# Attention with sorted limits: limits on GpSimd, four scalings on VectorE, and twelve products moved behind a branch

## The chip, the core and the metric

The kernel runs on one core of a Trainium2 chip. A core has five engines that run their own instruction lists and meet only at semaphores: TensorE (PE in the profile; PEld is its weight load), VectorE (DVE), ScalarE (ACT), GpSimd (POOL) and SyncE (SP), which here only issues DMAs. The metric is the device time of one execution in microseconds (us). Less is better.

## The reference

A decoder layer on 16 sequences of 256 tokens with 512 channels, f32: selective self-attention, a cross-attention, a feed-forward part, each followed by a residual add and a layer norm. Only the self-attention matters here:

```python
q_I = (x @ W_Iq).reshape(Bx, Tx, IH, DI); k_I = (x @ W_Ik).reshape(Bx, Tx, IH, DI)    # IH = 4
w = sigmoid(x @ W_Iw)
imp = w * sigmoid(einsum('bthd,bshd->bhts', q_I, k_I) + gate_bias)
imp = repeat(imp, H // IH, axis=1) * sigmoid(head_bias)                               # H = 16
k_t = clip(floor(K_BASE * var(causal imp) / variance_ema), K_MIN, K_MAX)
...
sel = the k_t keys of highest imp in each row (the first 4 keys always), causal
q, k = rotary(x @ W_q), rotary(x @ W_k);  v = x @ W_v * sigmoid(x @ W_gv)
attn = softmax(where(sel, q k^T / sqrt(32), -1e30))
out = (attn @ v) * sigmoid(x @ W_go) @ W_o
```

Each row of each head so has its own number of keys, and keeps those with the highest importance.

## The kernel before

**Stages.** After constants, `gates` (to about 343 us) computes w in a chain of exact products. `gate_sums` closes it: the sigmoid of w on VectorE, and beside it `project(0)`, the projections of the first sequence. Then `attention` computes, from w and the head bias, how many sorted keys any row can need, loads that flag into every engine (`values_load`, line 460) and branches to one of two bodies (`attend_all`, lines 461 to 464), which differ in the depth of the sort; the profiled execution takes the one of 64. From about 386 to 1790 us the body runs, then come the cross-attention and the feed-forward part, which the change does not touch.

**Projections.** `project(b)` is a generator. It makes 18 products in a fixed order: Iq, Ik, four of q, four of k, two of gv, four of go, two of v. Each takes two steps: the matmuls (a piece P of the plan), and ACT's copy out of PSUM (a piece C, line 599 or 643). After the fourth copy of q or k two DMAs on SP's queue (line 620) write the swapped pairs to `rot`, and three GpSimd instructions follow, one at each of the next copies: times cos (L621), rot times sin (L622), the add (L623), each over 128x1024. Sequence 0 is projected as a whole ahead of the branch; each later sequence in the slots of the sequence before it.

**Units.** A unit is one sequence with one of the four index heads, 64 in all; it serves four attention heads. Its work is cut into pieces that stand for: L logits (PE); G the gate, first on VectorE (L660), then Exp on ACT (L663), then plus one on GpSimd (L665); I reciprocal (VectorE, L673), times w (GpSimd, L677), statistics (VectorE, L683 to L688) and u (GpSimd, L690); V the four scalings of u by a head's factor, one piece per head (`scaled`, L704: 128x384, f32); R the sort with MAX8 and MATCH_REPLACE8 (L716, L718); N the counts (seven small GpSimd instructions, L726 to L733); T the thresholds (hits L749 on VectorE, L753 on GpSimd, then L757 to L773 with kseen); K the signs against the threshold (ACT, L781, with a sum per row); B the limit, `signs - k` (`limits`, L788, 8 elements a row); X and D transposes and the dropped keys (D on ACT, L815, takes the limit as bias); S scores; M maxima (L834); E exponentials (L842); Z scaling of p by 1/total (GpSimd, L851, eight instructions); A transposes of p and the product with v; U avs (ACT) times go (GpSimd, avT, L883); O the output projection, xs add (GpSimd, L898) and norm.

**Order.** The text `PLAN` (lines 54 to 59) is the order of one slot: `R1:3` is piece 1 of the sort for unit n+3. `attend_all` writes it out for slots n from -4 on and skips what doesn't exist yet, so that a slot holds pieces of several units; `in_order` then pins this order on PE, VectorE, ACT and GpSimd. SP keeps its own order of issue. A piece P or C in slot n advances the projection of sequence n//4 + 1 by one step, at position n%4 * 5 + k of its 18 products. In slots -4 to -1 there is nothing to do for P and C, since sequence 0 is already projected (`if 0 < b < B`, line 488). So n%4 tells which products and which norms lie in a slot: 0 the products from Iq to the third of q, and the norms of the sequence before; 1 the last of q and four of k, with q's rotation; 2 two of gv and three of go, with k's rotation; 3 the last of go and two of v.

The pieces around the change stand so in the plan:

```
R1:3 Z2:0 V2:2 P0:0 D2:1 V3:2 Z3:0 D3:1 C0:0 ... R2:3
... K3:2 S:1 ... M0:1 G1:4 X0:2 M1:1 T0:3 A4:0 U0:0 B:2 G2:4 O7:-2 U1:0 C2:0
I0:4 R6:3 ...
```

On VectorE, `V3` so comes behind `V2` with nothing between, and `B` stands between hits (T0) and the reciprocal (I0). On GpSimd, `V3` lies between the p scalings Z2 and Z3, and `B` comes ahead of gate L665 (G2). The fourth scaling (`j == 3`) is on GpSimd, the other three are on VectorE; the limit is on VectorE.

**Buffers.** Pool `pj` has two buffers per name unless a count is given, `p1` one. Sequence 0 takes Iq, Ik, qT, kT, goT and v from `p1`, later ones from `pj`. All xT come from one buffer in `xp`, so a sequence's load waits until the products of the one before are done.

Of the kernel before, what the change touches and what calls it, by code (L numbers as in the profile page):

```python
# [20 lines left out]
P = 128  # L21
# [5 lines left out]
KC = C // P  # L27
# [21 lines left out]
W_STEPS = (2.0**-9, 2.0**-17, 2.0**-25)  # L49
GS, GB = 8, 24  # L50
PIECES, SLOTS = 18, 5
VBUFS = 1

PLAN = """
# [8 lines left out]
class Kernel:  # L63
# [177 lines left out]
    def gate_steps(self, st, ps, c):  # L241
        nc, v = self.nc, self.nc.vector
        p1 = self.pool("g1", 1, stack=st)
        p2 = self.pool("g2", 2, stack=st)
        raw = {}
        for n in range(2):
            raw[n] = self.gate_load(p2, n)
        self.steps = self.t(p1, [P, 3], "gsteps")
        for k in range(3):
            v.memset(self.steps[:, k : k + 1], 1.5 * TWO23 * X_STEPS[k])  # L250
        self.minus = self.t(p1, [P, P], "minus", BF16)
        v.tensor_scalar_mul(self.minus, self.ident, -1.0)
        coef = self.gate_weights(p1)
        self.maskf = self.t(p1, [P, 32], "gmaskf")
        v.tensor_reduce(self.maskf, self.ident.rearrange("p (a q) -> p q a", a=4), AX.X, ALU.add)
        self.mask = self.t(p1, [P, 32], "gmask", BF16)
        v.tensor_copy(self.mask, self.maskf)
        big = self.t(ps, [P, C], "big")
        rest, t = (self.t(p1, [P, C], n) for n in ("rest", "t"))
        steps = C // 4  # L260
        starts = [0] + list(range(GS, steps, GB))
        blocks = [[self.t(p1, [P, GS, P], f"bd_first{k}", BF16) for k in range(5)]]
        for k in range(5):
            shape = [P, GS, 32, IH]
            v.tensor_tensor(
                blocks[0][k].rearrange("p j (q h) -> p j q h", h=IH),
                coef[k][:, 0:GS, :].unsqueeze(2).to_broadcast(shape),
                self.mask.unsqueeze(1).unsqueeze(3).to_broadcast(shape), op=ALU.mult)

        def new_block():  # L270
            blocks.append([self.t(p1, [P, GB, P], f"bd{k}", BF16, bufs=2) for k in range(5)])
            return self.gate_blocks(blocks[-1], coef, starts[len(blocks) - 1])

        def new_parts(n):
            parts[n] = self.t(p2, [P, GS, C], "xl", BF16, bufs=3)
            return self.gate_parts(p2, ps, raw.pop(n) if n in raw else self.gate_load(p2, n), parts[n])

        parts = {}
        for step in new_parts(0):
            pass  # L280
        stack = ExitStack()
        for ins in self.rounded:
            stack.enter_context(self.tc.issue_after(ins.ins))
        ahead = new_block(), new_parts(1)
        for n in range(20):
            next(ahead[0], None)
            if n % 3 == 2:
                next(ahead[1], None)
        for step in ahead[1]:
            pass  # L290
        stack.close()
        first = len(nc.cur_bb.bb.instructions)
        work = []
        self.W = {}
        loads = "W_Iq", "W_Ik", "W_q", "W_k", "W_gv", "W_go", "W_v"
        place = lambda j: (0, j) if j < GS else (1 + (j - GS) // GB, (j - GS) % GB)
        small = [self.gate_small(ps, blocks, place(0), parts[0], 0)]
        for j in range(steps):
            n, i = divmod(j, GS)
            if i == GS - 1 and n < len(loads):  # L300
                self.load_weight(loads[n])
            if j == 10 * GS:
                self.load_attention_constants(self.wp)
            if j == 12 * GS:
                self.xT0 = self.load_xT(0)
            if i == 0 and n + 2 < steps // GS:
                work.append(new_parts(n + 2))
            m, at = place(j)
            if at == 0 and m + 1 < len(starts):
                if m:  # L310
                    work.append(new_block())
            for k in range(2):
                self.add(big, blocks[m][k][:, at, :], parts[n][:, i, :], j == 0 and k == 0)
            if j + 1 < steps:
                small.append(self.gate_small(ps, blocks, place(j + 1), parts[(j + 1) // GS], (j + 1) % GS))
            if j == 0:
                v.tensor_copy(t, small.pop(0))
            else:
                v.tensor_add(t, rest, small.pop(0))  # L319
            v.tensor_add(c, t, big)  # L320
            if j + 1 < steps:
                v.tensor_sub(rest, c, big)  # L322
            work = [step for step in work if next(step, None)]
        self.in_order(first)
# [78 lines left out]
    def gate_sums(self, lanes):  # L403


        nc = self.nc
        v = nc.vector
        NO = NT * IH
        self.proj = {}
        made = self.project(0)  # L410
        step = lambda: next(made, None)
        with ExitStack() as st:
            pool = self.pool("g3", 1, stack=st)
            z = self.t(pool, [P, NO + H], "z")
            nc.scalar.dma_start(z[:, NO:], self.rows("head_bias", H))
            l5 = lanes.rearrange("p (n g l h) -> p l g n h", n=4, g=8, l=4)
            a, b = (self.t(pool, [P, 8, 4, IH], n) for n in ("za", "zb"))
            v.tensor_add(a, l5[:, 0], l5[:, 1])
            v.tensor_add(b, l5[:, 2], l5[:, 3])
            v.tensor_add(z[:, 0:NO].rearrange("p (g n h) -> p g n h", g=8, h=IH), a, b)  # L420
            self.load_weight("W_o")
            self.sigmoid(pool, z, self.wc, NO + H)
            for _ in range(2 * PIECES):
                step()
        self.first = self.proj[0]

    def load_x(self, pool, src):
# [38 lines left out]
    def attend_all(self, depth):  # L466

        self.depth = depth
        first = len(self.nc.cur_bb.bb.instructions)
        self.units = [(b, i) for b in range(B) for i in range(IH)]
        self.proj, self.sel = {0: self.first}, {}
        self.made = [self.project(b) for b in range(B)]
        plan = [(w[0], int("0" + w[1 : w.index(":")]), int(w[w.index(":") + 1 :])) for w in PLAN.split()]
        places = [off for _, _, off in plan]
        for n in range(min(-IH, -max(places)), len(self.units) - min(places)):
            for kind, k, off in plan:
                self.piece(kind, k, n + off)  # L480
        self.in_order(first)

    def piece(self, kind, k, n):

        if kind in "PC":

            b, at = n // IH + 1, n % IH * SLOTS + k
            if 0 < b < B and at < PIECES:
                next(self.made[b])
            return  # L490
        if not 0 <= n < len(self.units):
# [73 lines left out]

        self.nc.tensor.matmul(out, lhsT, rhs, start=start, stop=True, skip_group_check=True)  # L566

    def load_xT(self, b):
        xT = self.t(self.xp, [P, KC, T], "xT")
        self.nc.sync.dma_start(xT, self.ap["xT"].rearrange("(c p) n -> p c n", p=P)[:, :, b * T : (b + 1) * T])  # L570
        return xT

    def project(self, b):

        nc, W = self.nc, self.W
        v, g = nc.vector, nc.gpsimd
        r = self.proj[b] = {}
        pool = self.pj if b else self.p1
        if b == 0:
            xT = self.xT0  # L580
        else:
            xT = self.load_xT(b)
        gate = self.t(self.pj, [P, 2, C], "gate", bufs=1)
        later = []

        def product(name, c):
            ps = self.t(self.ps, [P, T], "mm", bufs=2)
# [12 lines left out]
            if later:  # L600
                later.pop(0)()

        for name in ("Iq", "Ik"):
            r[name] = self.t(pool, [P, T], name)
            ps = product(name, 0)
            yield
            copy(r[name], ps)
            yield
        turn = lambda a: a.unsqueeze(1).to_broadcast([P, KC, T])
        for name in ("q", "k"):  # L610
            out = r[name] = self.t(pool, [P, KC, T], name + "T")
            for c in range(KC):
                ps = product(name, c)
# [2 lines left out]
                if c == KC - 1:  # L616

                    rot = self.t(self.pj, [P, KC, T], "rot", bufs=1)
                    for k in range(2):
# [2 lines left out]
                                  lambda a=rot: g.tensor_mul(a, a, turn(self.sin)),  # L622
                                  lambda a=out, b=rot: g.tensor_add(a, a, b)))  # L623
                yield
        for i in range(2):
            ps = rows("gv", i)
            yield
            copy(gate[:, i, :], ps)
            yield
# [68 lines left out]
    def scaled(self, sel, j):  # L698

        if j == 0:  # L700
            sel["vv"] = self.t(self.sp, [P, HPI, SEG], "vv", bufs=VBUFS)
        h = sel["i"] * HPI + j
        eng = self.nc.gpsimd if j == 3 else self.nc.vector
        eng.tensor_scalar(sel["vv"][:, j, :], sel["u"], self.chf[:, h : h + 1], TINY,  # L704
                          op0=ALU.mult, op1=ALU.max)

    def sort(self, sel, part, parts):
# [75 lines left out]
                                      accum_out=sel["signs"][:, s, j : j + 1])  # L783

    def limits(self, sel):
        v = self.nc.vector
        sel["limit"] = self.t(self.sp, [P, 2, HPI], "limit")
        v.tensor_sub(sel["limit"], sel["signs"], sel["k"])  # L788

# [805 lines left out]
```

## Time and profile before

| | us |
|---|---|
| median of three runs | 3102.8 (3097.0 to 3104.5) |
| the profiled execution | 3102.2 |
| its span, first to last instruction | 3100.4 |
| `gates` | to 343 |
| sequence 0's products on PE | 343.5 to 383.2 |
| first reciprocal of the body | 386.6 |
| attention body | to about 1790 |
| cross-attention, feed-forward part | to 2400, to 3100 |
| four units in the middle (timeline, limit to limit) | 85.0 or 85.7, in turn |

The page's first part gives each engine's busy time and its share of the span. The second cuts the span into 40 slices of 77.5 us; a digit is the busy share in tenths. Windows give busy time per engine between two moments. In a timeline each line has start, duration, engine, line of the source, operation, the tile written and read, and, in brackets, how long the engine had been idle and what ended that. An instruction that cannot get at its data shows as a longer duration, not as idle time.

### The profile page before, as it was taken

The page shows a single profiled execution, that of the slowest core. Times are in us where ns is not written, and L with a number is a line of the kernel's source. Part 1 is how long each engine was busy: PE and PEld are TensorE (multiplying, and loading weights), DVE is VectorE, ACT ScalarE, POOL GpSimd, SP SyncE. Part 2 cuts the span into 40 slices and gives each one's busy share as a digit, 9 for nine tenths or more (in the row PEclk, how much of TensorE's full clock was granted, in tenths as well). Part 3 has the DMA queues.
Part 4 walks back from the last instruction along what each step waited for, and adds up shares of the span by engine and source line. Part 5 has one row for each costly group of instructions (what it writes and reads, how often), then busy time and mean ns, then how long its engine had stood idle before and what let it go on. Part 6 is the DMA issues. An engine that isn't in the chain of part 4 may idle for free.

```text
span 3100.4 us, 47026 instructions
## 1 busy us (share of the span) xinstructions
PE 2580.9 (83%) x15194; PEld 1511.3 (49%) x15270; DVE 2380.1 (77%) x6186; ACT 1829.9 (59%) x5175; POOL 1563.2 (50%) x2313
## 2 busy tenths in 40 slices
PE   5676849999999999999999757787876899798887
PEld 1222435656665665665566345555644444343333
DVE  6888599999999999999999467755453544577775
ACT  6765147877777877878777622454342444544442
POOL 5543247777777777777777424454333111012222
PEclk8999969999999999999999878888977899899999
DMA  3532100010010000001000053100100633233341
GB/s 100 140 110 64 41 9 16 35 35 35 28 35 35 35 28 21 32 31 35 35 35 28 15 191 125 39 1 5 25 21 14 232 149 142 109 109 136 113 145 55
DMA packets 85071, 200.83 MB, mean 65 GB/s; under 512 B 14160, under 2 KB 24144, under 8 KB 80720
## 3 DMA queue, kind: packets, MB, share of 16 engines
q1 hardware_dynamic: 69856, 148.17, 14.5%
q10 hardware_dynamic: 9840, 32.78, 3.2%
q0 software_dynamic: 5120, 16.78, 1.3%
q8 instruction: 123, 2.02, 0.3%
q14 instruction: 132, 1.08, 0.1%
HBM read 105.41 MB, written 58.72 MB: 53 GB/s over the span
## 4 chain that ended last, share of the span: by engine, by line
DVE 51%; PE 23%; issue 11%; POOL 10%; ACT 3%; DMA 2%; SPq 0%; DVEq 0%; ACTq 0%; POOLq 0%
PE mm L562 10%; DVE rest L718 9%; PE up L562 7%; DVE lists L716 7%; DVE gate L673 5%; DVE nmax L834 4%; DVE W_o L320 3%; DVE rest L322 3%; DVE t L319 2%; POOL rh L1164 2%; DVE vv L704 2%; DVE limit L788 2%; DVE hits L749 1%; DVE ln_s L913 1%; POOL p L851 1%
## 5 line engine op out<-in xcount | busy, mean ns | idle before, releaser
L562 PE MATMUL down<-wo,part 128*128 128x512 bf16 x1505 | 350.3, 392 | 55.6 <-DVE ln_a L915 21.7
L716 DVE MAX8 lists<-rest 128x8 f32<-128x128 f32 (+1 forms) x896 | 305.7, 347 | 0.0
L562 PEld LDWEIGHTS <-part 128*128 128x128 bf16 x1536 | 152.6, 101 | 253.4 <-DVE part L1464 47.8
L718 DVE MATCH_REPLACE8 rest<-lists,rest 128x128 f32<-128x128 f32 (+1 forms) x768 | 263.0, 342 | 0.0
L781 ACT ACTIVATE sign<-vv,thr 128x128 bf16<-128x128 f32 (+1 forms) x512 | 229.1, 452 | 35.5 <-DVE thr L771 34.9
L851 POOL TENSOR_SCALAR p<-p,total 128x128 f32<-128x128 f32 (+1 forms) x512 | 238.7, 483 | 14.9 <-DVE total L848 9.3
L815 ACT ACTIVATE drop<-w,limit 128x128 bf16<-128x128 f32 (+1 forms) x512 | 187.3, 453 | 84.8 <-PE w L562 52.1
L562 PE MATMUL up<-xT,wi 128*128 128x512 bf16 x1001 | 234.2, 393 | 2.2 <-ACT xT L1427 0.7
L1474 POOL TENSOR_TENSOR y<-y,xb 128x512 f32<-128x512 f32 x32 | 75.9, 2373 | 297.4 <-DVE y L1473 200.3
L842 ACT ACTIVATE p<-sc,nmax 128x128 f32<-128x128 f32 (+1 forms) x512 | 210.3, 440 | 4.1
L861 PE MATMUL w<-ident,p 128*128 128x128 f32 x768 | 161.3, 305 | 34.9 <-POOL p L851 22.8
L1440 DVE TENSOR_REDUCE hmax<-h 128x1 f32<-128x512 f32 x128 | 87.7, 686 | 131.6 <-ACT h L1438 131.6
L862 ACT COPY pT<-w 128x384 f32<-128x384 f32 x256 | 120.4, 480 | 98.6 <-PE w L861 95.2
L1438 ACT ACTIVATE h<-up,b_in,inv_in 128x512 f32<-128x512 f32 x128 | 99.4, 778 | 127.7 <-PE up L562 110.9
L562 PEld LDWEIGHTS <-wi 128*128 128x128 bf16 x1024 | 103.3, 101 | 127.6 <-issue 14.7
L673 DVE RECIPROCAL gate<-gate 128x384 f32<-128x384 f32 x64 | 162.8, 2544 | 1.7 <-POOL gate L665 1.4
L861 PEld LDWEIGHTS w<-ident,p 128*128 128x128 f32 x768 | 93.1, 146 | 133.4 <-POOL p L851 106.6
L1441 POOL DMA_DIRECT2D h<-h x64 | 35.0, 547 | 243.2 <-ACT h L1438 243.2
L566 PE MATMUL big<-xl,bd 128*128 128x512 bf16 x238 | 74.6, 395 | 85.4 <-DVE rest L322 83.7
L368 ACT ACTIVATE bd<-coef,gmaskf 128x96 bf16<-128x96 bf16 x500 | 137.1, 363 | 0.0
L562 PE MATMUL mm<-xT,W_k 128*128 128x256 f32 x512 | 134.0, 410 | 0.0
L1463 ACT CAST part<-hq 128x2048 bf16<-128x2048 f32 x32 | 60.7, 1897 | 121.8 <-POOL ln_a L916 52.8
(435 smaller groups left out, 7263.3 us busy)
## 6 DMA issues: line engine op xcount, KB each, us to landing
xl<-part SPq DMA_DIRECT2D x256, 64.0 KB, 2.0
h<-h POOLq DMA_DIRECT2D x64, 256.0 KB, 2.3
h<-h SPq DMA_DIRECT2D x64, 256.0 KB, 2.0
hq<-h ACTq DMA_DIRECT2D x16, 1024.0 KB, 4.8
hq<-h SPq DMA_DIRECT2D x16, 1024.0 KB, 4.8
xraw<-in_xg_dram SPq DMA_DIRECT2D x16, 512.0 KB, 3.4
xT<-in_xT_dram SPq DMA_DIRECT2D x16, 512.0 KB, 3.8
rot<-qT SPq DMA_DIRECT2D x32, 256.0 KB, 2.3
```

What stands on the lines that cost most here:

```text
L368: nc.scalar.activation(out[:, q], src, AF.Copy, scale=one)
L562: self.nc.tensor.matmul(out, lhsT, rhs, start=start, stop=stop)
L673: v.reciprocal(gate, gate)
L716: v.max(top, src)
L718: v.match_replace(sel["rest"][:, o : o + w], top, src, -4.0)
L781: self.nc.scalar.activation(sel["sign"][:, j, o : o + w], sel["vv"][:, j, o : o + w], AF.Sign, bias=sel["thr"][:, s, j : j + 1], scale=TWO ...
L815: nc.scalar.activation(sel["drop"][:, j, o : o + w], ps[:, o : o + w], AF.Relu, bias=sel["limit"][:, s, j : j + 1])
L834: v.tensor_reduce(nmax[:, s, :], sel["sc"][:, :, o : o + w], AX.X, ALU.max)
L842: self.nc.scalar.activation(sel["p"][:, j, o : o + w], sel["sc"][:, j, o : o + w], AF.Exp, bias=sel["nmax"][:, s, j : j + 1], scale=SCALE, ...
L851: self.nc.gpsimd.tensor_scalar(part, part, sel["total"][:, s, j : j + 1], 1.0, op0=ALU.mult, op1=ALU.mult)
L861: nc.tensor.transpose(ps[:, n * P : (n + 1) * P], sel["p"][:, j, n * P : (n + 1) * P], self.ident)
L862: nc.scalar.copy(pT[:, j, :], ps)
```

## The change

It does three things.
- `limits` runs on GpSimd in place of VectorE.
- `scaled` runs all four heads' instructions on VectorE.
- `gate_sums` steps through six products of sequence 0 (Iq, Ik, q) in place of 18, and issues q's rotation at once. The other twelve belong to `project(0, True)` in the body, which advances in slots -3 (k), -2 (gv, go) and -1 (go, v), at the same positions as for any later sequence. To that end k, go and v of sequence 0 come from `pj`, sequence 0 has an xT of its own in `xp`, and later xT come from one buffer in `pj`.

The plan's text is unchanged.

```diff
+FIRST = 6
...
-                self.xT0 = self.load_xT(0)
+                self.xT0 = self.load_xT(self.xp, 0)
...
-            for _ in range(2 * PIECES):
+            for _ in range(2 * FIRST):
                 step()
+            for f in self.later:
+                f()
         self.first = self.proj[0]
...
-        self.proj, self.sel = {0: self.first}, {}
-        self.made = [self.project(b) for b in range(B)]
+        self.proj, self.sel = {0: dict(self.first)}, {}
+        self.made = [self.project(b, b == 0) for b in range(B)]
...
-            if 0 < b < B and at < PIECES:
+            if b < B and (0 if b else FIRST) <= at < PIECES:
                 next(self.made[b])
...
-    def load_xT(self, b):
-        xT = self.t(self.xp, [P, KC, T], "xT")
+    def load_xT(self, pool, b):
+        xT = self.t(pool, [P, KC, T], "xT", bufs=1)
...
-    def project(self, b):
+    def project(self, b, begun=False):
...
-        pool = self.pj if b else self.p1
-        if b == 0:
-            xT = self.xT0
-        else:
-            xT = self.load_xT(b)
-        gate = self.t(self.pj, [P, 2, C], "gate", bufs=1)
-        later = []
+        pool = self.pj if b or begun else self.p1
+        xT = self.load_xT(self.pj, b) if b else self.xT0
+        later = self.later = []
...
-        for name in ("Iq", "Ik"):
+        for name in () if begun else ("Iq", "Ik"):
...
-        for name in ("q", "k"):
+        for name in ("k",) if begun else ("q", "k"):
...
+        gate = self.t(self.pj, [P, 2, C], "gate", bufs=1)
         for i in range(2):
             ps = rows("gv", i)
...
-        eng = self.nc.gpsimd if j == 3 else self.nc.vector
-        eng.tensor_scalar(sel["vv"][:, j, :], sel["u"], self.chf[:, h : h + 1], TINY,
+        self.nc.vector.tensor_scalar(sel["vv"][:, j, :], sel["u"], self.chf[:, h : h + 1], TINY,
                           op0=ALU.mult, op1=ALU.max)
...
     def limits(self, sel):
-        v = self.nc.vector
+        v = self.nc.gpsimd
```

More of the change, by code (lines that the diff above doesn't have):

```diff
@@ L566, in add @@
         self.nc.tensor.matmul(out, lhsT, rhs, start=start, stop=True, skip_group_check=True)
-    def load_xT(self, b):
-        xT = self.t(self.xp, [P, KC, T], "xT")
+    def load_xT(self, pool, b):
+        xT = self.t(pool, [P, KC, T], "xT", bufs=1)
         self.nc.sync.dma_start(xT, self.ap["xT"].rearrange("(c p) n -> p c n", p=P)[:, :, b * T : (b + 1) * T])
         return xT
-    def project(self, b):
+    def project(self, b, begun=False):
         nc, W = self.nc, self.W
         v, g = nc.vector, nc.gpsimd
-        r = self.proj[b] = {}
-        pool = self.pj if b else self.p1
-        if b == 0:
-            xT = self.xT0
-        else:
-            xT = self.load_xT(b)
-        gate = self.t(self.pj, [P, 2, C], "gate", bufs=1)
-        later = []
+        r = self.proj.setdefault(b, {})
+        pool = self.pj if b or begun else self.p1
+        xT = self.load_xT(self.pj, b) if b else self.xT0
+        later = self.later = []
         def product(name, c):
```

## The prediction

> **What bounds the kernel now.** I read the page's busy shares and 40 slices first, then the windows by stage, the waits in 500 to 1700 us, and then, engine by engine, the timeline of a few units.
>
> ```profile
> PE 2580.9 (83%) x15194; PEld 1511.3 (49%) x15270; DVE 2380.1 (77%) x6186; ACT 1829.9 (59%) x5175; POOL 1563.2 (50%) x2313
> DVE  6888599999999999999999467755453544577775
> 1000.00:1100.00 100.00, 95.48 (x599) 62.66 (x598) 95.67 (x306) 81.02 (x270) 78.77 (x118) 0.98 0.08 28
> ```
>
> The change touches 343 to 1790 us. There VectorE (DVE) is busy 95.7 of 100 us, and in the waits of 500 to 1700 us it lacks something for only 13.2 us (gate L660, for the logits). PE shows 95.5, but its rows start-to-start, at full clock, add up to 74 us of work in a sequence of 85 (14 products of 1.73, 4 of 3.44, two W_o products of 3.44, four units of 7.4). So VectorE's list sets the pace. Part of its busy time is not work:
>
> ```profile
> 1156.51 2.43 DVE L749 TENSOR_TENSOR hits<-rank,count 128x264 f32<-128x264 f32 x1
> 1158.86 2.30 DVE L788 TENSOR_TENSOR limit<-signs,kseen 128x8 f32<-128x8 f32 x1
> 1161.09 2.54 DVE L673 RECIPROCAL gate<-gate 128x384 f32<-128x384 f32 x1
> ...
> 1156.29 2.36 POOL L622 TENSOR_TENSOR rot<-rot,sin 128x1024 f32<-128x1024 f32 x1
> 1158.73 2.41 POOL L623 TENSOR_TENSOR qT<-qT,rot 128x1024 f32<-128x1024 f32 x1
> ```
>
> The limit is 8 elements a row and takes 0.15 us where GpSimd is idle. Here it takes 2.30 and ends with GpSimd's multiply: an instruction of VectorE with two SBUF inputs stands still while GpSimd is inside one of its own. hits, in front of it, pays 2.0 in the same way. By the timelines the 64 units repeat in fours, one sequence, about 85.3 us. I number them by the slot n%4 of the plan; limit takes
> slot 0: 0.15; slot 1: 2.30; slot 2: 0.69 (avT L883 in GpSimd); slot 3: 0.47 (gate L665 in GpSimd).
> The reciprocal and MAX8 never stretch.
>
> **Part 1, the limit leaves VectorE.** What is late next, slot by slot:
> - Slot 0: start to next start is 0.08; that comes back.
> - Slot 1: 2.22 to 2.24 come back, since the reciprocal doesn't stretch and its gate is ready 4.1 us (every second sequence 1.8 us) earlier. In those second sequences the sin multiply sits under the limit itself (1073.14), and the rotation's add would then still hold GpSimd until 1077.9, behind which L677 of the next stage queues; statistics would wait some 0.85. So 2.2 and 1.4, mean 1.8.
> - Slot 2: 0.53 over its own 0.08. But hits will meet avT instead, which waits for ACT's avs and does not move; I count 0.2 net, with part 2 in it.
> - Slot 3: nothing. GpSimd's gate ends at the reciprocal's start (0.02 us before), and it hangs on ACT.
> On GpSimd the limit costs about 0.20 (row of L729, the same 8 elements), behind the last sign and ahead of gate L665. Gate waits for ACT's Exp, which ACT does after the signs, so the limit fits into that wait in slots 0, 1 and 3 (1.4 to 4.2 us of idle); in slot 2 GpSimd comes straight from sin, but 1.67 earlier than now (part 2). ACT's drop gains: it waits 28.4 us for the limit now, 14 times, up to 3.2.
>
> **Part 2, the fourth scaling.** GpSimd loses 1.59 us plus 0.08 per unit. VectorE gains an instruction right behind the third scaling:
>
> ```profile
> 1020.25 0.41 DVE L704 TENSOR_SCALAR vv<-u,chf 128x384 f32<-128x384 f32 x1
> 1020.58 0.29 DVE L716 MAX8 lists<-rest 128x8 f32<-128x128 f32 x1
> ...
> 1039.33 1.43 DVE L704 TENSOR_SCALAR vv<-u,chf 128x384 f32<-128x384 f32 x1
> 1040.69 0.28 DVE L716 MAX8 lists<-rest 128x8 f32<-128x128 f32 x1
> ```
>
> It costs 0.33 from start to start if it runs at once. Two such in a row, with GpSimd in its p scalings (L851), are nowhere in the trace. Under the third scaling a p op starts at +0.03 and ends at +0.65; if the fourth has to wait for its end, the next start is 0.15 later (as behind L898, which ended at 1040.54), so it costs 0.47. Highest: another whole p op, 0.8. Below zero it cannot be, as the instruction is new. I take 0.47, since a p op was in flight there in nearly every unit I looked at. The Trainium skill, page "SBUF — State Buffer", section "Who interferes with whom", says that whichever of the two engines issues first holds the shared ports for the whole instruction and that an fp32 tensor_scalar between SBUF tiles can take both; by it the fourth scaling waits, which is the 0.47, and with 0.33 the sum would be some 3 us lower. The 1.43 above agrees.
>
> What covers it: in slot 3 VectorE idles 0.61 before L660 (PE's logits) and the reciprocal hangs on ACT; in slot 1 hits ends with the sin multiply however late it starts (long form) or with avT (short); in slot 2 with avT. In slot 0 nothing covers it; a later hits only misses avT and saves 0.16. If the cover fails in slots 1 to 3, that is 1.4 more in each four units. Per four units: slot 0 +0.47 - 0.08 - 0.16 = +0.2; slot 1 -1.8; slot 2 -0.2; slot 3 0. That is -1.8, and 15 such fours run between 455 and 1733 us: **-27**. The first three units have neither stalls nor cover: 3 x (0.47 - 0.08) = **+1.2**. In the end run the transposes of the last heads wait for GpSimd's p behind its scaling (1.46 us before 1726.91); I take **-1**.
>
> **Part 3, the front.**
>
> ```profile
> 357.50 0.15 DVE L459 TENSOR_SCALAR few<-top 128x1 int32<-128x1 f32 x1
> 383.24 0.33 PE L562 MATMUL w<-unseen,neg_ident 128*128 128x384 bf16 x1
> 386.56 2.55 DVE L673 RECIPROCAL gate<-gate 128x384 f32<-128x384 f32 x1 [1.42 <-POOL gate L665]
> 363.98 2.35 POOL L623 TENSOR_TENSOR qT<-qT,rot 128x1024 f32<-128x1024 f32 x1
> ```
>
> VectorE knows the body at 357.65 and has branched at 358.7, but the first logits queue on PE behind 12 products until 383.24, and the first reciprocal starts at 386.56. After, PE is through with the first six at 355.8. The branch then ends at 358.7 on the engines, logits, VectorE's gate and ACT's Exp with its table load (1.28) take until some 361.5. GpSimd is later: the three q rotations, now issued at once ahead of its branch, start when the two rot DMAs have landed (359.25) and end at 366.33. Gate L665 (0.51) then gives a reciprocal at some 366.95: **-19.6**.
>
> The 12 products are not gone: 4 x 1.73 in slot -3, 12.1 us in slot -2, 8.6 in slot -1, beside 14 to 19 us of VectorE work each; PE is busy there 35.6 of the 76 us from 384 to 460. With them go their 12 copies on ACT (0.37 to 0.59), two sigmoids with table loads, three k rotations (7.1) and two v products (1.27) on GpSimd, and two rot DMAs on SP (1.1 us to issue). On SP nothing waits behind these but the next xT, which gets a buffer of its own and no longer waits for PE. The rotations can hold up hits or a scaling as in slot 1, 2.4 at most each. And PE's clock is low there (0.50 in 400 to 420): at that clock eight matmuls took 3.59 instead of 1.89, and 24 us of products would overrun slot -2 by 7. Bounds 0 and 8; I take **+3**, near the stalls of one slot, because PE gets 40 us of dense work. The Trainium skill, "TensorE: Matmul & The Clock Gate", "What's actually happening", has the clock return after one busy window of about 3.4 us; by it the 7 would not be paid, and the trace agrees as far as the granted clock goes back to 0.94 in 440 to 460, when products begin.
>
> **Sum.** -27 + 1.2 - 1 - 19.6 + 3 = -43. The profiled execution took 3102.2 us (span 3100.4), the median of the runs is 3102.8; forecast **3059**. Its own range: parts 1 and 2 between -40 (0.33 paid, slots 1 and 2 all returned) and -8 (0.8 paid, half covered), part 3 between -11.6 and -19.6: 3042 to 3082.
>
> **Rivals.**
> - A, the second loop binds: agg L688, GpSimd's counts and p, PE's transposes, signs, Exp, gate, reciprocal. In slot 3 it takes 14.0 of 20.1 us (1016.23 to 1030.21) and leaves VectorE 1.0 spare. If it binds in slots 1 and 2 too, VectorE's saving turns into waits before L660 or L673 and only the front is left: 3102 - 17 - 1 = 3084. For it: PE's 95%. Against it: in slot 1 the gate is ready 1.8 to 4.1 us early, and ACT waits for VectorE's limit and thr.
> - B, more comes back: GpSimd is 1.67 earlier in every unit. If xs L898 also stops meeting L688, kseen and the scalings (0.8 to 1.1 each, once or twice a sequence), a sequence gives 4.5 instead of 1.8: 3102 - 68 - 17 = 3017. Against it: L898 follows ACT's copies, not the scaling.
> - C, slower: the fourth scaling loses the port to all three p ops in a row, until 1021.7 instead of 1020.9: 1.42 in each of 64 units, +91. Limits give back 2.9 x 15 = 43 and the front 17: +30, 3132. It decides from 0.95 us per unit. Against it: no scaling of the trace waits for more than the op in flight.
> - D, the front doesn't move (the branch waits for code, or logits still for products): 3102 - 27 = 3075. Against it: ACT issued 0.1 us after its branch.
>
> **How the numbers follow.** Forecast 0.62, A 0.16, B 0.09, C 0.05, D 0.05, and 0.03 that gains vanish altogether. Three runs here span 7 us, so 0.3% (9 us) is about what a measurement tells from no change. Faster: the forecast, A, B and D, 0.90 with the thin edge of A taken off; slower 0.05, same 0.05. The range takes the forecast's own, A and D, and a little of B's side: 3035 to 3088.
>
> **What would show it.** First reciprocal near 367; four units in about 83.5 instead of 85.3; L788 on GpSimd at 0.2 with no wait of drop for it; 256 scalings on VectorE at 0.41 with every fourth near 0.55; in slot 1 a reciprocal directly behind hits. It is wrong if hits or the fourth scaling take over the limit's wait in another slot, or if L660 or L673 show new idle time.

## The result, and the profile after

The changed kernel takes 3086.26 us (median of 8 runs, 3077.01 to 3089.26), the kernel before 3100.91 (8 runs, 3097.01 to 3104.48): ratio 0.995, 95% interval 0.9938 to 0.9962, 14.65 us less. It is faster, by a third of the 43 us forecast. The profiled execution took 3089.26 us, its span is 3087.5, so 12.9 less than the profiled execution before.

Line numbers shift by a few from kernel to kernel: hits is L749 before, L748 in the change and L753 in e4. The same lines as in the prediction, two from the page:

```profile
PE 2589.3 (84%) x15270; PEld 1512.9 (49%) x15270; DVE 2390.7 (77%) x6186; ACT 1827.6 (59%) x5175; POOL 1463.6 (47%) x2313
DVE  6888799999999999999999477654553454567775
```

One from the windows (length, then PE, PEld, DVE, ACT, POOL, granted clock, DMA share, GB/s):

```profile
1000.00:1100.00 100.00, 94.16 (x566) 58.91 (x564) 96.26 (x319) 80.13 (x255) 66.34 (x121) 0.97 0.10 33
```

GpSimd lost 99.6 us of busy time (1563.2 to 1463.6). VectorE, which the 64 limits have left, has 10.6 us more. 256 scalings on VectorE instead of 192 explain 64 x 0.41 = 26 of busy time; the limits took away 58 (0.15, 2.30, 0.69 and 0.47 in turn, 16 times). So some 40 us of busy time are new on VectorE and are neither. In the middle VectorE is still busy 96.3 of 100 us, and it waits for anything at all in 500 to 1600 us for only 5.2 us (reciprocal, for gate L665). Its list still sets the pace, and the list still stands still. Slot 1 and slot 2 of one sequence, VectorE's timeline first:

```profile
1058.77 1.83 DVE L748 TENSOR_TENSOR hits<-rank,count 128x264 f32<-128x264 f32 x1
1060.52 2.54 DVE L673 RECIPROCAL gate<-gate 128x384 f32<-128x384 f32 x1
...
1079.35 2.09 DVE L748 TENSOR_TENSOR hits<-rank,count 128x264 f32<-128x264 f32 x1
1081.36 2.54 DVE L673 RECIPROCAL gate<-gate 128x384 f32<-128x384 f32 x1
```

GpSimd's timeline at the same time:

```profile
1057.28 0.73 POOL L882 TENSOR_TENSOR avT<-avs,goT 128x256 f32<-128x256 f32 x1 [0.20 <-ACT avs L880]
1057.96 2.35 POOL L621 TENSOR_TENSOR rot<-rot,sin 128x1024 f32<-128x1024 f32 x1
...
1077.05 0.20 POOL L787 TENSOR_TENSOR limit<-signs,kseen 128x8 f32<-128x8 f32 x1
1077.22 0.51 POOL L665 TENSOR_SCALAR gate<-gate 128x384 f32<-128x384 f32 x1
1078.11 0.72 POOL L882 TENSOR_TENSOR avT<-avs,goT 128x256 f32<-128x256 f32 x1 [0.38 <-ACT avs L880]
1078.79 2.36 POOL L622 TENSOR_TENSOR kT<-kT,rot 128x1024 f32<-128x1024 f32 x1
```

In slot 1 all is as forecast: hits ends 0.3 after the sin multiply (1060.31), and the reciprocal is directly behind. In slot 2 hits takes 2.09, and it ends 0.3 after the rotation's **add** (1081.15), not with avT. The same place before, VectorE's timeline first:

```profile
1009.03 0.64 DVE L749 TENSOR_TENSOR hits<-rank,count 128x264 f32<-128x264 f32 x1
1009.59 0.69 DVE L788 TENSOR_TENSOR limit<-signs,kseen 128x8 f32<-128x8 f32 x1
1010.20 2.54 DVE L673 RECIPROCAL gate<-gate 128x384 f32<-128x384 f32 x1
```

GpSimd's timeline at the same time:

```profile
1008.88 0.51 POOL L665 TENSOR_SCALAR gate<-gate 128x384 f32<-128x384 f32 x1
1009.36 0.90 POOL L883 TENSOR_TENSOR avT<-avs,goT 128x256 f32<-128x256 f32 x1
1010.22 2.36 POOL L623 TENSOR_TENSOR kT<-kT,rot 128x1024 f32<-128x1024 f32 x1
```

There hits took 0.64, and the add began at 1010.22, when the reciprocal (2.54 to 2.55 in all rows shown) had begun at 1010.20. Now the add is in front of hits.

Where the time went, over the whole body, from reciprocal to reciprocal (mean of the steady sequences; before, the interval into slot 1 was 22.3 or 23.0):

| us | before | after | difference | forecast |
|---|---|---|---|---|
| first reciprocal, from the span's start | 386.56 | 369.48 | -17.1 | -19.6 |
| first four units | 68.85 | 74.44 | +5.6 | +3 and +1.2 |
| interval into slot 1 | 22.6 | 20.65 | -2.0 | -1.8 |
| into slot 2 | 19.7 | 20.85 | +1.15 | -0.2 |
| into slot 3 | 20.0 | 19.8 | -0.2 | 0 |
| into slot 0 | 23.0 | 23.8 | +0.8 | +0.2 |
| four units | 85.3 | 85.1 | -0.2 | -1.8 |
| last reciprocal to the end of the span | 1388.8 | 1390.1 | +1.4 | -1 |

The second kind of count used below is how long VectorE's instructions stand still: for each instruction of a unit's list the time from its start to the next start, less the shortest such time of the same instruction, summed over four units. Before it is 8.27 us (limit 3.10, hits 1.68, rest 3.49), after 7.18 (hits 3.85, with 0.4 that is really the reciprocal's wait in slot 3; kseen 1.20; rest 2.13). Without that wait, hits has taken over some 1.8 of the limit's 3.1. With the list of instructions unchanged, this count and the time of four units must move together, since the count is that time less a fixed sum; what it tells is in which rows the time lies.

### The profile page after: what moved, and what is told of

It is laid out like the page before. It is cut to its first block, busy times and chain, and to the rows that moved or that the text cites. A ratio compares the mean times of both kernels' runs of the same rounds, so it can differ in the third digit from the quotient of the medians.

```text
span 3087.5 us, 47136 instructions
## 1 busy us (share of the span) xinstructions
PE 2589.3 (84%) x15270; PEld 1512.9 (49%) x15270; DVE 2390.7 (77%) x6186; ACT 1827.6 (59%) x5175; POOL 1463.6 (47%) x2313
## 4 chain that ended last, share of the span: by engine, by line
DVE 52%; PE 22%; issue 10%; POOL 9%; ACT 4%; DMA 2%; SPq 0%; DVEq 0%; POOLq 0%; ACTq 0%
DVE rest L717 10%; PE mm L565 8%; DVE lists L715 7%; PE up L565 7%; DVE gate L673 5%; DVE nmax L833 3%; DVE vv L703 3%; DVE W_o L321 3%; DVE rest L323 2%; DVE t L320 2%; DVE hits L748 2%; POOL rh L1163 2%; DVE ln_s L912 2%; POOL y L1473 1%; ACT p L1295 1%
## 5 line engine op out<-in xcount | busy, mean ns | idle before, releaser
L565 PEld LDWEIGHTS <-wi 128*128 128x128 bf16 x1024 | 103.8, 101 | 129.2 <-issue 17.6
L569 PE MATMUL big<-xl,bd 128*128 128x512 bf16 x240 | 76.7, 403 | 83.6 <-DVE rest L323 82.0
L915 POOL TENSOR_TENSOR ln_a<-ln_a,half_neg 128x1 f32<-128x1 f32 x98 | 55.6, 567 | 176.2 <-DVE ln_a L914 172.0
L565 PE MATMUL mm<-xT,W_k 128*128 128x256 f32 x512 | 126.2, 391 | 11.9 <-ACT kT L598 11.9
```

Source lines behind the costliest of these rows:

```text
L565: self.nc.tensor.matmul(out, lhsT, rhs, start=start, stop=stop)
```

## The experiments

Three theories. **T**: standing still moved from the limit to hits, because GpSimd, 1.6 us of scaling lighter per unit, reaches its long two-input instructions earlier, and VectorE reaches hits later. **P**: the fourth scaling simply costs more on VectorE than I took. **L**: the second loop (rival A: PE, ACT or GpSimd) takes what VectorE gave back.

### The parts alone

```diff
e1_limit, on the kernel before:
-        v = self.nc.vector            # limits
+        v = self.nc.gpsimd
e2_scale, on the kernel before:
-        eng = self.nc.gpsimd if j == 3 else self.nc.vector
-        eng.tensor_scalar(sel["vv"][:, j, :], ...
+        self.nc.vector.tensor_scalar(sel["vv"][:, j, :], ...
e3_front: the change without these two
```

> The kernel before with the limit alone moved to GpSimd; the fourth scaling stays on GpSimd and all 18 products stay ahead of the branch. Theory T (the limit's 3.1 us of standing still in four units do come back, and in the changed kernel hits lost 2.2 of them again, because GpSimd runs 1.6 us earlier and VectorE later): without the shift hits keeps its 1.7 us in four units, so four units take some 85.3 - 2.6 = 82.7 and the time falls by 30 to 40 us to some 3065. Theory P (the limit's return is whole, and the fourth scaling's price on VectorE ate it): the same, 3065. Theory L (PE, ACT and GpSimd form a second loop that keeps four units at 85): 3095 to 3101, with new idle time before L660 or L673.

> The kernel before with the fourth scaling alone moved to VectorE. Theory P: 0.5 us or more in each unit, +30 to +45 us, with the fourth scaling's own duration well above 0.41. Theory T: 0.33 to 0.55 for the scaling itself, and hits and the limit together stand still longer than the 4.8 us in four units of before, since the rotations come 1.6 us earlier: +20 to +40 us, with the excess over 64 x 0.33 = 21 in hits and limit. Theory L: under +10.

> The kernel before with only the twelve products moved behind the branch. The front itself should give 17 to 19.6 us up to the first reciprocal, and slots -3 to -1 should take 3 to 6 back through the k rotation meeting the scalings and hits: 3101 - 14 = 3087, between 3082 and 3091, for all theories; if it is so, the two other edits together are worth nothing in the changed kernel. Four units stay at 85.0 and 85.7 in turn.

Beside 3100.37 of the kernel before:

| | us | ratio, 95% interval | four units | standing still of limit, hits |
|---|---|---|---|---|
| limit alone | 3063.60 | 0.9875 (0.9857 to 0.9892) | 82.8 | 0, 2.5 |
| scaling alone | 3138.43 | 1.0119 (1.0098 to 1.014) | 87.7 | 4.1, 2.2 |
| front alone | 3082.61 | 0.9946 (0.9929 to 0.9963) | 85.3 | 3.1, 1.9 |

The limit gives 37, the front 18, and the scaling **costs 38**. They add up: -37 + 38 - 18 = -17, against -14.65 measured. So the gain went into the fourth scaling alone; the front and the limit did what they were to do (four units 2.5 shorter; first reciprocal at 366.82, where 366.95 was forecast for this order of events). That 38 is far over 64 x 0.47 = 30, and with the cover that the prediction counted on, nothing of it should have shown outside slot 0. In e2 the limit too stands longer: in slot 2 it takes 2.31 in 11 of 15 sequences, where it took 0.69. P and T are not yet told apart.

### GpSimd held back

```diff
e4_hold, on the changed kernel, behind the scalings:
+        if j == 3:
+            spare = self.t(self.sp, [P, SEG], "spare", bufs=1)
+            self.nc.gpsimd.tensor_scalar(spare, sel["u"], self.chf[:, h : h + 1], TINY,
+                                         op0=ALU.mult, op1=ALU.max)
e5_limit_front, on the changed kernel: the fourth scaling back on GpSimd
```

e4 does the fourth scaling twice, once on VectorE as in the change and once more on GpSimd at the old place, into a tile that nobody reads.

> The changed kernel, with a scaling of the same size added on GpSimd at the old place of the fourth (its result is not used), so that GpSimd's rotations come as late as before. It only adds work. Theory T: in slot 2 the rotation's add no longer comes ahead of hits, hits stands still 1 to 1.4 us less in four units, and the kernel gets faster by some 10 to 20 us, to 3066 to 3076. Theory P: VectorE's list is the same, so 3086, or slower by a few us. Theory L: slower, since GpSimd's p scaling of the last head comes 1.6 us later.

> The changed kernel with the fourth scaling put back on GpSimd, so the limit's move and the front together. Theory T and theory P: the single moves add up (limit -37, scaling +38, front -18 so far), so 3100 - 37 - 18 = 3045, between 3040 and 3052, with four units at some 82.8. Theory L, in the form that the changed kernel's front left no slack for it: 3055 or more.

e4 took 3066.17 (3100.37 before; 0.9886, 0.9865 to 0.9906): 64 more instructions of 1.59 us on GpSimd, and it is **20 us faster** than the change. Slot 2 of e4, VectorE's timeline:

```profile
985.36 0.47 DVE L753 TENSOR_TENSOR hits<-rank,count 128x264 f32<-128x264 f32 x1
985.75 2.54 DVE L673 RECIPROCAL gate<-gate 128x384 f32<-128x384 f32 x1
```

GpSimd's timeline at the same time:

```profile
977.75 1.59 POOL L708 TENSOR_SCALAR spare<-u,chf 128x384 f32<-128x384 f32 x1
...
985.51 0.90 POOL L887 TENSOR_TENSOR avT<-avs,goT 128x256 f32<-128x256 f32 x1
986.37 2.35 POOL L622 TENSOR_TENSOR kT<-kT,rot 128x1024 f32<-128x1024 f32 x1
```

The useless scaling holds avT and the add back until the reciprocal runs; hits takes 0.47. Starts in this slot, in us after slot 1's reciprocal, the same within 0.1 in six sequences of each (but one of the change, where avT, the add and hits come 0.3 later):

| | GpSimd k's cos | gate L665 | avT | add L622 | VectorE hits | next reciprocal |
|---|---|---|---|---|---|---|
| before | 13.7 | 18.4 | 18.85 | 19.7 | 18.5 | 19.7 |
| change | 11.9 | 16.7 | 17.6 | 18.3 | 18.8 | 20.85 |
| e4 | 13.7 | 18.5 | 19.0 | 19.85 | 18.8 | 19.2 |

Hits comes at the same moment in e4 and in the change; GpSimd alone differs. The interval into slot 2 is 19.2 instead of 20.85, and four units take 83.93 instead of 85.14. Of the standing still, hits falls by 1.6, and the scalings rise by 0.4. Neither P nor L makes added work a gain; T does. e5 took 3048.28 (3103.68 before; 0.9822, 0.9806 to 0.9839). Between e4 and e5 lies the fourth scaling on VectorE with GpSimd's order the same: 17.9 us, 0.28 a unit, by medians from two chips; the four units differ by 1.1 (83.93 and 82.80), the first four by 4.2. This is P's part. So of the 38, 20 go when GpSimd is as late as before, and 18 stay with the scaling on VectorE. Some 2 of these 18 are a meeting as well: in slot -2 of e4 the fourth scaling takes 2.51 (at 391.75) beside k's cos (391.57, 2.47).

### Where hits stands

```diff
e6_hits_late, on the changed kernel, in the plan:
-... X0:2 M1:1 T0:3 A4:0 U0:0 B:2 G2:4 O7:-2 U1:0 C2:0
-I0:4 R6:3 ...
+... X0:2 M1:1 A4:0 U0:0 B:2 G2:4 O7:-2 U1:0 C2:0
+I0:4 T0:3 R6:3 ...
e7_three: e6, with the fourth scaling back on GpSimd
e8_add_late, on the changed kernel: C2:0 behind I0:4
```

> The changed kernel with hits (T0) moved in the plan from ahead of the reciprocal to right behind it; no work is added or taken away. Theory T: in slot 2 the rotation's add has ended before the reciprocal ends, so hits gives back some 1.7 us there; in slot 1 it still meets the add for some 1.6: four units 1.5 to 2 us shorter, 3056 to 3064. Theory P: within 5 us of 3086, as the fourth scaling stays where it is.

> Limit on GpSimd, front moved, fourth scaling on GpSimd, and hits behind the reciprocal: what the theory would choose. Hits stands still 2.5 us in four units without the last edit; it should fall to 1.6 or so (the add in slot 1 stays), and slot 3 keeps its wait for gate L665: 3033 to 3045.

> The changed kernel with the piece C2 moved behind the reciprocal, so that in slot 2 the rotation's add, and in slot 1 its sin multiply, are issued behind it on GpSimd's list and behind ACT's work of that place. Theory T: hits gives back 1.6 us in slot 2 and up to 1.4 in slot 1, of which some 1 is lost again as GpSimd's times w (L677) then queues behind two rotations: 3056 to 3066. Theory P: 3086 or slower.

All beside 3103.68 of the kernel before. e6: 3056.91 (0.9856, 0.984 to 0.9872), four units 83.3, hits 1.5 of standing still, as T had it. e7: 3042.94 (0.9807, 0.9791 to 0.9824). e8: 3084.81 (0.9937, 0.9921 to 0.9954), hits 3.81.

e7 came within its range, but not in the way expected. Its four units take 83.0, against 82.8 in e5, which has hits in the old place; hits stands still 2.1 instead of 1.6, as it meets more of the add in slot 1 than in e6 (it takes 2.26, in e6 1.80), and the reciprocal waits 8.9 us for gate L665 in 500 to 1600 us (5.6 in e5). With the fourth scaling on GpSimd, hits behind the reciprocal so brings nothing in the steady units; e7 is 5 us below e5 outside them (first four units 68.3, in e5 70.6).

e8 was a failed edit. It was to put the add behind the reciprocal, but I0 is one instruction on VectorE alone, so that moving a GpSimd piece past it changes no engine's list. It says nothing for or against T; it serves as a repeat of the change on the chip of e5 to e7. Against it e6 is 28 faster with the same instructions, only one of them 2.5 us later on VectorE.

### Hits early, and the add taken out

```diff
e9_hits_early, on the changed kernel, in the plan:
-... R5:3 O6:-1 M0:1 G1:4 X0:2 M1:1 T0:3 A4:0 ...
+... R5:3 O6:-1 T0:3 M0:1 G1:4 X0:2 M1:1 A4:0 ...
e10_best: e9, with the fourth scaling back on GpSimd
e11_no_add, on the changed kernel: L622 only for q, so that k stays without
the second half of its rotation
```

> The changed kernel with hits (T0) ahead of the two maxima on VectorE's list, 1.7 us earlier; the same instructions in all. In the trace of the changed kernel GpSimd is between its two-input instructions there in all four slots. Theory T: hits stands still under 0.6 us in four units in place of 3.85, four units some 2.5 to 3.3 us shorter, 3036 to 3050, if the gate in slot 3 does not hold the reciprocal longer. Theory P: 3081 to 3091.

> Limit on GpSimd, front moved, fourth scaling on GpSimd, hits ahead of the maxima. Theory T: of the 2.5 us that hits stands still in four units here, 1.5 to 2.2 come back, unless PE and ACT now hold VectorE before L660 and L673: 3015 to 3030. Theory L, which has not shown itself so far, would show here first: 3040 to 3048 and new idle time before L660.

> The changed kernel without the last instruction of k's rotation (L622, the GpSimd add of the sin part for k, 2.36 us once in four units), so that part of the rotation is left out of the computation. Theory T: the add is what holds up hits in slot 2; without it slot 2's stage falls from 20.8 to some 19.2 us, 3058 to 3066. Theory P: GpSimd has idle time there, so 3083 to 3088.

Beside 3102.07 of the kernel before:

| | us | ratio, 95% interval | four units | standing still, all | of it hits |
|---|---|---|---|---|---|
| hits early | 3013.34 | 0.9729 (0.9703 to 0.9755) | 80.3 | 2.33 | under 0.15 |
| hits early, scaling on GpSimd | 3013.61 | 0.9714 (0.9688 to 0.974) | 80.3 | 3.73 | 1.26 |
| without k's add | 3058.69 | 0.9862 (0.9843 to 0.9882) | 83.6 | 5.69 | 2.11 |

e11 takes out the add itself, and the interval into slot 2 falls from 20.85 to 19.2 or 19.5, with hits at no more than its own time there: T by a second way. Here GpSimd has less to do, in e4 more; both free hits, both give 20 to 28 us.

e9 gave more than the 3036 to 3050 expected. Hits falls by 3.85, kseen by 1.1, agg by 0.62, and some 0.8 goes into other rows: standing still is 4.85 less. Slot 0 of the change, VectorE's timeline:

```profile
1025.14 1.27 DVE L772 TENSOR_TENSOR kseen<-kseen,seen 128x8 f32<-128x8 f32 x1
```

GpSimd's timeline at the same time:

```profile
1025.11 1.27 POOL L897 TENSOR_TENSOR xs<-xs,oc 128x512 f32<-128x512 f32 x1
```

Eight elements a row, 1.27 us, until the residual add ends. In e9 these adds come at other moments, under MAX8 and MATCH_REPLACE8, which pay nothing (a scaling at the end of one pays 0.35); kseen takes at most 0.19 in 950 to 1060 us, where it took up to 1.27. The group of hits in that stretch, in the change (shortest, median, longest in ns; first and last start):

```profile
L748 DVE TENSOR_TENSOR hits<-rank,count x6: 426/1280/2091, 953.7 to 1058.8; 128x264 f32<-128x264 f32 x6
```

The same row of e9:

```profile
L748 DVE TENSOR_TENSOR hits<-rank,count x6: 422/423/424, 959.1 to 1059.0; 128x264 f32<-128x264 f32 x6
```

Four units take 85.14 - 80.26 = 4.88 us less; 15 of them make 73 us, and the medians differ by 73. That the count of standing still falls by the same is no support by itself, since it must. What supports T is where it falls: in hits, kseen and agg, which read two tiles of SBUF each, and not in the reciprocal, the maxima or the sort. I had not foreseen that kseen and agg would come free with hits: that is a by-product of the new phase.

That e9 and e10 are equal is no proof that the fourth scaling is free. e9 does 4 x 0.33 = 1.3 more on VectorE, and e10 stands still 1.4 longer (3.73 against 2.33), since with its scaling GpSimd is late again and hits, now earlier, meets k's sin multiply in slot 2 (hits 956.77 to 958.76, the multiply 956.12 to 958.47). The two cancel. e10 took 1.4 us less than its range, though only 1.2 of hits' 2.5 came back and not 1.5 to 2.2: here too kseen and agg gave 1.7 more.

## Why the prediction was right and wrong, point by point

- **What bounds the kernel: right.** In 500 to 1600 us VectorE lacks something for 5.2 us in the change and for 6.1 in e9.
- **Part 1, right.** Slot 1's interval fell by 2.0 (1.8 forecast), hits ending with the sin multiply and the reciprocal behind it. On GpSimd the limit takes 0.20 (median 201 ns of 64), and ACT's drop no longer waits for it. Alone, it brought 37. One reading is wrong: the limit's 2.30 at 1158.86 ends (1161.16) with the rotation's add (1161.14), not with the multiply; it is hits that ends just behind the multiply (1158.65). The sum does not hang on it.
- **Part 2, slot 2: wrong, and the step that failed.** "But hits will meet avT instead, which waits for ACT's avs and does not move; I count 0.2 net, with part 2 in it." It was +1.15: 1.35 us a sequence off, 20 us in fifteen. avT did move, by 1.25 (18.85 to 17.6), and the add by 1.45, to 0.55 ahead of hits. avT did not wait for avs before: from the scaling's start at 1001.76 on, GpSimd's rows follow each other without a gap through cos, sin, gate and avT to the add, so it hung on GpSimd's own queue, which the change shortens. Only now is there a gap before avT (0.38, ended by avs). I had the number in hand, "1.67 earlier than now (part 2)", for the gate of the same slot, and did not carry it two instructions on. An earlier GpSimd was counted as a gain only.
- **Part 2, slot 0: the size was off.** +0.2 was forecast, +0.8 came. The third and the fourth scaling there stand 0.2 each behind p ops, and kseen 0.42 longer under the residual add, as in e1 and e2 too.
- **Part 2, the price of the scaling.** I took 0.47, between 0.33 and 0.8, by a p op in flight. Measured: 0.33 in three slots of four, 0.55 in slot 0. VectorE's timeline in two slots of the change:

```profile
1091.49 0.74 DVE L703 TENSOR_SCALAR vv<-u,chf 128x384 f32<-128x384 f32 x2
...
1113.26 1.16 DVE L703 TENSOR_SCALAR vv<-u,chf 128x384 f32<-128x384 f32 x2
```

Each line is the third and fourth together; 0.74 is two at full pace, 1.16 are two that each stood 0.2. In the first, a p op (128x256) took 0.90 instead of 0.47: GpSimd waited, not VectorE. The Trainium skill, page "SBUF — State Buffer", section "Who interferes with whom", leaves open which of the two waits and makes it depend on who issued first; the trace shows both outcomes. That the order of issue decides it does not show: in slot 0 the scaling that waits has the earlier recorded start (1113.26, the p op 1113.29). I had drawn from it that the scaling waits, which is only one of the two. The cover I gave it in slots 1 to 3 was partly false: 18 us of price between e4 and e5, of which 4.2 lie in the first four units.

- **The first units: somewhat too small.** +5.6 instead of +4.2. The front alone shows +2.0 (forecast 3); the scalings add the rest, and by the same mechanism: in slot -2 GpSimd, with no scaling of its own ahead, starts k's cos just before VectorE's second scaling. GpSimd's timeline:

```profile
391.80 2.35 POOL L620 TENSOR_TENSOR kT<-kT,cos 128x1024 f32<-128x1024 f32 x1
```

VectorE at that moment:

```profile
391.85 2.52 DVE L703 TENSOR_SCALAR vv<-u,chf 128x384 f32<-128x384 f32 x1
```

In e5 the cos comes at 392.56, after the start of VectorE's last scaling (392.39), and that takes 0.41.

- **Part 3, right.** In the forecast order: q's last rotation, gate L665, reciprocal. VectorE's timeline:

```profile
360.10 0.15 DVE L462 TENSOR_SCALAR few<-top 128x1 int32<-128x1 f32 x1
...
369.48 2.55 DVE L673 RECIPROCAL gate<-gate 128x384 f32<-128x384 f32 x1 [6.15 <-POOL gate L665]
```

From the flag to the reciprocal it is 9.4 us, as worked out (357.50 to 366.95). In this execution the flag itself came 2.6 later than before; over the other kernels with the new front, the first reciprocal lies between 365.9 and 369.3. The upper bound of 8 for the first units, a PE clock as low as before, did not come: with the products there the granted clock is 0.91 in 384 to 400 and in 400 to 420, where it was 0.62 and 0.50.

- **Rivals.** A gave 3084, next to the 3086 measured, but its mechanism is not there: VectorE's waits got fewer, not more, and e4, with more on GpSimd, is faster. A number that fits is no sign that the reason holds. B's 3017 is nearly what e9 reaches, by its mechanism (nothing meets any more), but only with the plan changed. C is excluded: no steady scaling stood 1.42 (the longest by far, 2.52, is under a cos in slot -2). The closing sentence named the failure ("if hits or the fourth scaling take over the limit's wait in another slot"), and the rivals gave it no time and no chance of its own. It should have been one: hits paying in slot 2 what it paid in slot 1, 1.2 to 2.0 a sequence, 18 to 30 us, makes 3077 to 3089.

The sum by its terms, on the profiled executions: steady units -27 forecast, about -3 measured (24 off); first reciprocal 2.5 off; first units 1.4; the end 2.4. From the last reciprocal to the last residual add of the attention it is 69.4 before and 69.2 after; what is behind it lies in stages that the change does not touch, and takes 1313.2 to 1322.2 in the kernels run here.

What stays open: why the residual adds fall on kseen in the change and not in e9 is shown as moments, not tested by itself; it was not tried to move them alone.

## What to carry to other kernels

Where two engines block each other by meeting, work taken off the one that is not the bound moves its later instructions earlier, and each of them can come to lie on a blockable instruction of the bound: lay the two timelines over each other again with both shifts before you count the gain, and give "the same stall under another instruction" a chance of its own. A piece in an order written by hand that can be blocked is best placed where the other engine is idle or does nothing long: moving one piece of VectorE's list two maxima forward brought 73 us, five times what the whole change brought. Look for such stalls in durations (shortest, median, longest of one group), since no list of waits shows them.

## What the runs showed that was not expected

- Work added to an engine made the kernel faster: 64 x 1.59 us on GpSimd, 20 us less in all (e4 against the change).
- When a scaling on VectorE and a p scaling on GpSimd overlap, either may pay: in three slots VectorE's scalings take 0.33 each and GpSimd's p op 0.90 instead of 0.47; in the fourth the scalings take 0.53 and 0.55, and the p ops 0.37 and 0.57.
- In the rows shown, the blocked time does not go by the size of the blocked instruction; it lasts until GpSimd's instruction ends. 8 elements a row took 1.27 us beside an add of 1.27 begun 0.03 earlier, 264 elements 2.09 beside one of 2.36 begun 0.56 earlier.
